# A six-layer window-attention stack: the closing normalization moves to ScalarE, and the planner gets other durations, delays and priorities

## The chip, the core and the metric

The kernel runs on one core of a Trainium2 chip. The core has a matrix engine (TensorE, PE in the profile, with its weight loads shown apart as PEld), a vector engine (VectorE, DVE), an activation engine (ScalarE, ACT), a general-purpose engine (GpSimd, POOL) and a queue that issues the transfers (SyncE, SP). Each engine works through its own list of instructions in order. An instruction that needs the result of another engine waits for a semaphore, and everything behind it on its engine waits too. The metric is device time in microseconds (us), the median of several runs. The profile comes from one execution with the hardware profiler on.

## What is computed

Sixteen sequences of 256 tokens, 128 features wide, all in 32-bit floats, go through four blocks, each followed by a residual sum and a normalization over the features. The first three blocks (linear attention, a mixture of eight experts, a causal attention with softmax feature maps) form the first stage of the kernel, which the change doesn't touch. The fourth block is the six-layer stack. Cut to what matters:

```python
def attn_layer(x, Wqkv, qs, ksc, Wo):              # 16 heads of 64
    q, k, v = split(x @ Wqkv)
    q, k = l2norm(q) * qs, l2norm(k) * ksc
    q = q * cos * scale + rotate_half(q) * sin * scale
    k = k * cos / scale + rotate_half(k) * sin / scale
    out = local_attention(q, k, v)                 # each block of 32 sees itself and the block before
    return out @ Wo
def ffn_layer(x, g, bln, W1, b1, W2, b2):
    xn = normalized(x) * g + bln
    a, gate = split(xn @ W1 + b1)
    return a * gelu(gate) @ W2 + b2
for i in range(6):
    x = attn_layer(shift_tokens(x), ...) + x
    x = ffn_layer(shift_tokens(x), ...) + x
out = _layernorm(x_in + x)                         # the closing normalization
```

## The kernel before

**Units and tiles.** Two sequences make a unit, so there are 8 units; a sequence has two tiles of 128 tokens, so a unit has 4. The stack keeps each unit's activations in SBUF for all six layers, transposed (features on partitions), in `xs`.

**Two stages.** The first stage, planned by a `Plan` of its own, ends near 1085 us of the span. The second stage is the stack: for each layer, each unit: two sequences through `projections`, `rotations`, `windows`, `attention` and `output`, then one `feed_forward` for the unit. After the last layer each unit goes through `final`, which transposes it back, adds the kept input and normalizes it.

**The planner.** The program isn't written in the order in which it runs. Every piece of work is a `Step` with an engine, a duration in us (`work`), the steps that must come first, the buffers it takes and those it uses. `Plan.run` is a list scheduler on the host: it steps through a modelled time; whenever an engine is free it issues, of the steps whose predecessors are done in the model and whose buffers are free, the one with the lowest rank. A step counts as done `work` plus the engine's `LAG` after its start. The rank is the number of the tile (so older tiles go first) plus a due time by kind plus an entry of the dictionary given to `Plan` (a negative entry makes a kind of step more urgent; 1.0 is worth one tile). The durations, delays and ranks decide nothing at run time. They decide the order in which each engine's instructions are written down, and which buffer each step gets. The chip then runs that order with its own durations and waits.

**Buffers that bind.** The stack shares four PSUM buffers of two banks each (`pair`) between all products, transposes and mixes; five `t1` and two `t2` buffers hold the two halves of the rotation, and `final` takes one of each from its first step to its last.

**One tile, with the lines of the profile.** The projection (L1086, two for a tile: q and k) writes a `pair`. Three steps read it: `second` (VectorE, L1100), `first` (VectorE, L1093) and `square` (ScalarE, L1107). The model has no dependency among these three readers. `squares` (L1113) sums the squares, `rotated` (GpSimd, L1110) adds the two halves, `norms` (GpSimd, L1063 to L1071) makes the inverse norms, `scale` (GpSimd, L1156) applies those of k. `turn` (L1160) transposes on TensorE, `put` (L1166) copies out on ScalarE. `scores` (L1234), then `mask` (L1242) and `top` (L1256) on VectorE, `below` on GpSimd (L1264), `exps` on ScalarE (L1268, four groups of four heads), `total` on VectorE (L1275, L1276), `divide` on GpSimd (L1279), `turn` on VectorE (L1283), `mix` on TensorE (L1293, into two `pair` buffers) and its `put` on ScalarE (L1302). `output` is L1341 and L1350, `windows` L1210 and L1213, `feed_forward` L1367 to L1434. `join` multiplies the value and output weights of a layer ahead of time.

**The end.** `final` of a unit gathers on ScalarE (L1542), transposes on TensorE (L249), adds on VectorE (L1551), takes statistics on VectorE (L1557, L1559), the inverse root on GpSimd (L1563, L228), normalizes on VectorE (L1568, four instructions of 128x128) and writes out through SP (L1574).

Of the kernel before, what the change touches and what calls it, by code (L numbers as in the profile page):

```python
# [16 lines left out]
P = 128  # L17
# [182 lines left out]
def tile_kernel(ctx: ExitStack, tc: tile.TileContext, a: dict, out: bass.AP):  # L200
# [26 lines left out]
    def rsqrt(o, i, n):  # L227
        pool.tensor_tensor(o, i, nhalf.to_broadcast([P, n]), ALU.pow)  # L228
# [759 lines left out]
    with ExitStack() as st:  # L988
# [26 lines left out]
        for kT in slots["kT"]:  # L1015
# [6 lines left out]
            "attention.divide": 0.5,  # L1022
            "attention.below": 8,
            "projections.first": 0.5,
# [3 lines left out]
            "windows.turn": 3,  # L1028
# [6 lines left out]
            "attention.exps": 4.5,  # L1035
            "feed_forward.turn_back": -6,
            "attention.total": 1.5,
            "feed_forward.inner": 2,
            "join.product": 1,
            "attention.put": 4,  # L1040
            "rotations.scale": 2,
        })

# [104 lines left out]
        def rotations(q):  # L1148
# [21 lines left out]
            nm = step("pool", 5.3, norms, q.reds, [], [q.ss], q.rank + due["norms"])  # L1170
# [4 lines left out]
        def turned(q, t, nm, scale, turn, put):  # L1175
# [5 lines left out]
            for qk in range(2):  # L1181
# [4 lines left out]
                else:  # L1186

                    m = o.adds[qk]
                tn = step("pe", 0.95, partial(turn, o.t1s[qk], pz), [m], [pz], [o.t1s[qk]], rank + due["rotated"], count=16)
# [3 lines left out]
                        "act", 0.91, partial(put, dst, off, pz), [tn], new,  # L1193
# [6 lines left out]
        def windows(q):  # L1200
# [15 lines left out]
            tn = step("pe", 0.5, turn, [*q.ready, begun], [pz, q.xw], [], rank + due["windows"], count=8)  # L1216
            q.spread = step("act", 0.6, put, [tn], [], [pz, q.xw], rank)

        def attention(q, t):
# [93 lines left out]
            mk = step("dve", 1.13, mask, sc, [e], [pS], rank + due["mask"])  # L1313
            tp = step("dve", 1.13, top, [mk], [], [e], rank + due["top"])
            be = step("pool", 0.35, below, [tp, o.normed], [], [], rank)
            ex = [step("act", 1.36, partial(exps, g), [be], [], [e], rank, ("exp", 0)) for g in range(4)]
            q.soft.append(tp)
            sm = step("dve", 1.46, total, ex, [], [e], rank)
            dv = step("pool", 1.87, divide, [sm], [], [e], rank)
            te = step("dve", 1.24, turn, [dv], [eT], [e], rank + due["turn"])  # L1320
            if t == 0:
# [4 lines left out]
                "pe", 2.27, partial(mix, ps), [te, q.spread, *q.mixed], [*ps, *new],  # L1326
# [3 lines left out]
            for g in range(2):  # L1330
                q.outs.append(
                    step("act", 0.91, partial(put, g, ps[g]), [mx], [], [ps[g], q.zT], rank)
                )
# [22 lines left out]
        def feed_forward(u, w, after, loaded, rank):  # L1356
# [80 lines left out]
            sx = step("dve", 1.3, stats, [tn], [], [px], rank)  # L1437
# [5 lines left out]
            for c in range(len(FCH)):  # L1443
                pg = Buf("pair")
                gm = step("pe", 0.92, partial(inner, 1, c, pg), [af], [pg], [xn], rank + due["ff_inner"])
# [79 lines left out]
        def final(u, after, rank):  # L1525
# [7 lines left out]
            def tile_of(b, j):  # L1533
                return half(b, 1)[:, j * P : (j + 1) * P]
# [141 lines left out]
```

## Time and profile before

| What | us |
|---|---|
| median of 3 runs | 4286.88 (4279.67 to 4288.96) |
| the profiled execution | 4283.78 |
| its span, first to last instruction | 4281.5 |
| TensorE busy | 4026.8 (94%) |
| VectorE busy | 3540.7 (83%) |
| ScalarE busy | 3147.6 (74%) |
| GpSimd busy | 2692.0 (63%) |
| first stage, about | 0 to 1085 |

The mean granted TensorE clock of the execution is 0.988 of full speed. The transfers are few: 37.03 MB over the whole span, a mean of 9 GB/s.

The page lists busy time by engine, a strip of 40 slices, the queues, the chain of work that ended last, and the groups of instructions with their idle time before and who ended it. Beside it the trace can be asked for waits between pairs of lines, for the instructions in order of time, and for busy times in chosen windows. A useful clock for the second stage is the first instruction of `outer` in `feed_forward` (L1422), once for a unit and layer, 48 times in all. The starts in the second layer are at 1873.73, 1941.05, 2005.20, 2068.64, 2133.26, 2197.61, 2261.95 and 2326.29 us, and in the last layer at 3941.76, 4009.06, 4087.69, 4157.76, 4218.76, 4250.92, 4260.72 and 4268.03 us.

### The profile page before, as it was taken

How to read it: one execution, taken by the hardware profiler on the slowest of the kernel's cores; microseconds unless marked ns; L12 is line 12 of the kernel's file. 1: busy time of each engine (PE TensorE's matmuls, PEld its weight loads, DVE VectorE, ACT ScalarE, POOL GpSimd, SP SyncE). 2: the span in 40 equal slices, each digit the busy share in tenths (PEclk: the TensorE clock that was granted, in tenths of full speed). 3: DMA queues.
4: the chain of work that ended last, by engine and by line, in shares of the span. 5: the costliest groups of instructions: out<-in, count | busy, mean ns of one | idle time of the engine just before them, and what ended most of it. 6: DMA issues, size and time to landing. Idle time of an engine off the chain costs nothing.

```text
span 4281.5 us, 104658 instructions
## 1 busy us (share of the span) xinstructions
PE 4026.8 (94%) x43728; PEld 2666.5 (62%) x43728; DVE 3540.7 (83%) x5201; ACT 3147.6 (74%) x6106; POOL 2692.0 (63%) x2865
## 2 busy tenths in 40 slices
PE   8999999999799999999999999999999999999888
PEld 5777777787455555565565565565555565555555
DVE  6888888787688888888888888888888888888886
ACT  6766766665478778787778777778787787777675
POOL 2654555566676676667666666766666666766662
PEclk9999999999899999999999999999999999999999
DMA  3000000000000000000000000000000000000000
GB/s 89 4 6 6 4 1 4 3 4 3 20 2 11 2 13 2 7 12 2 13 2 7 11 2 13 2 7 12 2 13 2 7 12 2 2 2 4 9 7 25
DMA packets 30836, 37.03 MB, mean 9 GB/s; under 512 B 5406, under 2 KB 24348, under 8 KB 29596
## 3 DMA queue, kind: packets, MB, share of 16 engines
q1 hardware_dynamic: 30364, 30.35, 2.4%
q8 instruction: 343, 5.62, 0.6%
q14 instruction: 129, 1.06, 0.1%
HBM read 26.15 MB, written 4.19 MB: 7 GB/s over the span
## 4 chain that ended last, share of the span: by engine, by line
PE 54%; DVE 25%; POOL 9%; ACT 8%; issue 4%; SPq 0%; DMA 0%; ACTq 0%; POOLq 0%; DVEq 0%
PE pp L1086 10%; PE pp L1341 8%; PE pp L1160 6%; DVE d_t L1093 5%; DVE d_t L1100 5%; PE pp L1402 4%; ACT d_sq L1107 4%; PE pp L1293 4%; DVE d_e L1242 3%; POOL d_e L1279 3%; PE pp L1234 3%; POOL d_t L1110 2%; PE pp L1422 2%; PE pb L665 2%; DVE d_eT L1283 2%
## 5 line engine op out<-in xcount | busy, mean ns | idle before, releaser
L1110 POOL TENSOR_TENSOR d_t<-d_t,d_t 128x1024 f32<-128x1024 f32 x384 | 904.4, 2360 | 770.0 <-DVE d_t L1093 734.1
L1268 ACT ACTIVATE d_e<-d_e,d_m,d_ny 128x64 f32<-128x64 f32 x3072 | 1071.3, 433 | 90.6 <-POOL d_m L1264 90.0
L1086 PE MATMUL pp<-d_wqkv,xs 128*128 128x512 f32 x1536 | 731.8, 609 | 12.5 <-DVE d_e L1242 6.7
L1341 PE MATMUL pp<-d_zT,d_wvo 128*128 128x256 f32 x3072 | 685.7, 381 | 7.5 <-DVE d_t L1093 2.8
L1100 DVE TENSOR_TENSOR d_t<-pp,d_tab 128x1024 f32<-128x1024 f32 x384 | 467.4, 1218 | 220.6 <-ACT d_sq L1107 126.9
L1341 PEld LDWEIGHTS pp<-d_zT,d_wvo 128*128 128x128 f32 x3072 | 577.8, 191 | 89.5 <-ACT d_sq L1107 8.6
L1107 ACT ACTIVATE d_sq<-pp 128x1024 f32<-128x1024 f32 x384 | 389.0, 1022 | 313.6 <-DVE d_t L1093 102.8
L1302 ACT COPY d_zT<-pp 128x1024 f32<-128x1024 f32 x384 | 373.2, 1012 | 235.1 <-PE pp L1293 235.1
L1093 DVE TENSOR_TENSOR d_t<-pp,d_tab 128x1024 f32<-128x1024 f32 x384 | 465.4, 1213 | 61.7 <-ACT d_sq L1107 61.6
L1113 DVE TENSOR_REDUCE d_ss<-d_sq 128x16 f32<-128x1024 f32 x384 | 455.0, 1201 | 6.4 <-ACT d_sq L1107 5.2
L1293 PE MATMUL pp<-d_eT,d_xw 32*128 32x512 f32 x3072 | 434.1, 618 | 26.2 <-ACT f_xn L1396 17.2
L1160 PE MATMUL pp<-ident,d_t 128*128 128x128 f32 x3072 | 409.4, 280 | 49.3 <-DVE d_t L1093 30.7
L1086 PEld LDWEIGHTS pp<-d_wqkv,xs 128*128 128x128 f32 x1536 | 276.2, 192 | 272.5 <-issue 225.2
L1234 PEld LDWEIGHTS pp<-d_kT,d_qT 64*32 64x32 f32 x24576 | 238.6, 106 | 329.8 <-issue 296.1
L1160 PEld LDWEIGHTS pp<-ident,d_t 128*128 128x128 f32 x3072 | 340.9, 143 | 144.2 <-issue 57.7
L1279 POOL TENSOR_TENSOR d_e<-d_e,d_z 128x1024 f32<-128x1024 f32 x192 | 365.1, 1902 | 46.5 <-DVE d_z L1276 43.0
L1156 POOL TENSOR_TENSOR d_t<-d_t,d_ny 128x1024 f32<-128x1024 f32 x192 | 363.2, 1903 | 0.4
L855 POOL TENSOR_TENSOR c_e<-c_e,c_sm 128x1024 f32<-128x1024 f32 x128 | 248.7, 1950 | 178.1 <-DVE c_sm L851 125.0
L1234 PE MATMUL pp<-d_kT,d_qT 64*32 64x64 f32 x24576 | 333.6, 224 | 8.0 <-ACT d_kT L1166 4.5
L1283 DVE STREAM_TRANSPOSE d_eT<-d_e 128x1024 f32<-128x1024 f32 x192 | 237.6, 1238 | 105.3 <-POOL d_e L1279 105.2
L1402 PE MATMUL pp<-f_xn,d_w 128*128 128x512 f32 (+1 forms) x576 | 276.5, 605 | 29.5 <-DVE d_e L1242 27.8
L1293 PEld LDWEIGHTS pp<-d_eT,d_xw 32*128 32x128 f32 x3072 | 156.4, 184 | 186.8 <-issue 87.8
(184 smaller groups left out, 7252.5 us busy)
## 6 DMA issues: line engine op xcount, KB each, us to landing
d_wqkv<-L_ffn_Wqkv SPq DMA_DIRECT2D x6, 1024.0 KB
d_t<-L_ffn_Wqkv SPq DMA_DIRECT2D x10, 256.0 KB
d_t<-L_ffn_Wo SPq DMA_DIRECT2D x10, 256.0 KB, 3.5
a_xin<-L_attn_x SPq DMA_DIRECT2D x8, 256.0 KB, 2.9
keep<-bc_x SPq DMA_DIRECT2D x8, 256.0 KB, 2.0
d_t<-keep SPq DMA_DIRECT2D x8, 256.0 KB, 3.9
out<-d_t SPq DMA_DIRECT2D x8, 256.0 KB, 2.3
d_w<-L_ffn_W SPq DMA_DIRECT2D x6, 341.0 KB
```

Of the source, the lines that this page charges most:

```text
L1086: pe.matmul(pj.t[:, hf * 512 : (hf + 1) * 512], lhsT=xj, rhs=q.w["qkv"][:, c : c + 512], start=True, stop=True,)
L1093: dve.tensor_tensor(t1.t, heads(pj.t), bc(q.lay.tab[:, 0, t, cc], hs, 1), ALU.mult)
L1100: dve.tensor_tensor(t2.t.rearrange("p h (x d) -> p h x d", x=2), swapped(pj.t), bc(q.lay.tab[:, 1, t, cc].rearrange("p (x d) -> p x d", x= ...
L1107: act.activation(sq.t, heads(pj.t), AF.Square)
L1110: pool.tensor_tensor(t1.t, t1.t, t2.t, ALU.add)
L1113: dve.tensor_reduce(q.ss.t[:, t, qk, :], sq.t, AX.X, ALU.add)
L1160: pe.transpose(pz.t[:, c * P : (c + 1) * P], t1.t[:, 2 * c : 2 * c + 2, :].rearrange("p h d -> p (h d)"), ident,)
L1234: pe.matmul(pS.t[b * WIN : (b + 1) * WIN, s0 : s0 + 2 * WIN], lhsT=qT.t[r, c, b * WIN : (b + 1) * WIN], rhs=kT.t[r, c, k0 : k0 + 2 * WIN], ...
L1268: act.activation(each()[:, h, :], each()[:, h, :], AF.Exp, bias=o.m[:, h : h + 1], scale=norm_of(h),)
L1279: pool.tensor_tensor(each(), each(), bc(o.z, es, 2), ALU.mult)
L1293: pe.matmul(ps[b // 2].t[:, (b % 2) * 512 : (b % 2 + 1) * 512], lhsT=q.xw.t[r, 2 * t + j, :], rhs=eT.t[r, j, :, :].rearrange("p h n -> p ( ...
L1341: pe.matmul(pr.t[:, :SEQ], lhsT=q.w["vo"][:, (h % 2) * 8 + h // 2, :], rhs=q.zT.t[:, :, h, :], start=(h == 0), stop=(h == HEADS - 1),)
```

## The change

The change has two parts, both in the second stage.

The last step of `final` moves: four `tensor_scalar` instructions on VectorE (subtract the mean, multiply by the inverse root) become four `activation` instructions on ScalarE with the function Identity (scale by the inverse root, add a bias). The bias, minus mean times inverse root, is made by two more small instructions on GpSimd.

The second planner gets another table of priorities, other delays, and other durations for some steps. The first planner keeps all of its own.

```diff
             "attention.mix": -0.5,
-            "attention.divide": 0.5,
-            "attention.below": 8,
-            "projections.first": 0.5,
+            "attention.divide": 2.5,
+            "attention.below": 11,
+            "projections.first": -1.0,
...
-            "windows.turn": 3,
+            "windows.turn": 3.5,
...
-            "attention.exps": 4.5,
+            "attention.exps": 7.5,
             "feed_forward.turn_back": -6,
-            "attention.total": 1.5,
+            "attention.total": 3.0,
             "feed_forward.inner": 2,
-            "join.product": 1,
-            "attention.put": 4,
-            "rotations.scale": 2,
+            "attention.put": 6,
+            "rotations.scale": 3,
+            "projections.square": -0.5,
         })
+        plan.LAG = {"pe": 0.12, "act": 0.1, "dve": 0.13, "pool": 0.1, "sp": 2.5}
```

Before, `LAG` was pe 0.27, act 0.17, dve 0.2, pool 0.1, sp 2.5. The durations, old and new, in us:

| step | engine | old | new |
|---|---|---|---|
| `rotations.norms` | GpSimd | 5.3 | 5.2 |
| `rotations.turn` | TensorE | 0.95 | 1.0 |
| `rotations.put` | ScalarE | 0.91 | 0.9 |
| `windows.turn`, `windows.put` | TensorE, ScalarE | 0.5, 0.6 | 0.55, 0.5 |
| `attention.mask` | VectorE | 1.13 | 1.19 |
| `attention.below` | GpSimd | 0.35 | 0.25 |
| `attention.exps` | ScalarE | 1.36 | 1.34 |
| `attention.total`, `attention.turn` | VectorE | 1.46, 1.24 | 1.42, 1.17 |
| `attention.mix` | TensorE | 2.27 | 2.05 |
| `attention.put` | ScalarE | 0.91 | 0.9 |
| `feed_forward.stats`, `gated`, `add` | VectorE | 1.3, 0.7, 1.55 | 1.06, 0.66, 1.46 |
| `feed_forward.inner`, `outer` | TensorE | 0.92, 2.58 | 0.87, 2.67 |
| `final.gather` | ScalarE | 1.1 | 1.26 |
| `final.root` | GpSimd | 1.32 | 1.9 |
| `final.normal` | VectorE, then ScalarE | 1.4 | 1.3 |

And the moved step:

```diff
             def root():
                 o.rs = sd.tile([P, TPU], F32, name="f_rs")
+                o.nb = sd.tile([P, TPU], F32, name="f_nb")
                 pool.tensor_scalar(o.rs, o.mv[:, :, 1], EPS, None, ALU.add)
                 rsqrt(o.rs, o.rs, TPU)
+                pool.tensor_tensor(o.nb, o.mv[:, :, 0], o.rs, ALU.mult)
+                pool.tensor_scalar(o.nb, o.nb, -1.0, None, ALU.mult)
 
             def normal():
                 for j in range(TPU):
-                    dve.tensor_scalar(
-                        tile_of(b2, j), tile_of(b1, j), o.mv[:, j, 0:1], o.rs[:, j : j + 1],
-                        ALU.subtract, ALU.mult,
+                    act.activation(
+                        tile_of(b2, j), tile_of(b1, j), AF.Identity,
+                        bias=o.nb[:, j : j + 1], scale=o.rs[:, j : j + 1],
                     )
```

## The prediction

> **What bounds the kernel now.** I read the busy line and the chain first.
>
> ```profile
> PE 4026.8 (94%) x43728; PEld 2666.5 (62%) x43728; DVE 3540.7 (83%) x5201; ACT 3147.6 (74%) x6106; POOL 2692.0 (63%) x2865
> PE 54%; DVE 25%; POOL 9%; ACT 8%; issue 4%; SPq 0%; DMA 0%; ACTq 0%; POOLq 0%; DVEq 0%
> ```
>
> TensorE is nearly always occupied, yet holds only half of the chain: VectorE carries a quarter. So I looked at one unit of the stack. The starts of `outer` (L1422) repeat every 64.34 us in the middle of each layer. A table of busy time over one such unit and over two of the last layer:
>
> ```profile
> core 0: us, PE busy (x) PEld busy (x) DVE busy (x) ACT busy (x) POOL busy (x), PEclk, DMA share, GB/s
> 2586.09:2650.43 64.34, 61.39 (x771) 37.11 (x770) 54.73 (x66) 50.24 (x96) 43.97 (x50) 1.00 0.06 20
> 4009.06:4087.69 78.63, 70.31 (x797) 43.11 (x795) 63.88 (x88) 51.61 (x94) 44.76 (x53) 0.93 0.03 8
> 4087.69:4157.76 70.07, 61.98 (x756) 38.19 (x755) 61.24 (x70) 52.64 (x104) 45.84 (x51) 0.93 0.03 9
> ```
>
> A steady unit leaves TensorE 64.34 - 61.39 = 2.95 us idle and VectorE 9.6. The list of TensorE's waits inside that unit names 2.6 us of this, in four places:
>
> ```profile
> PE pp L1210 <- DVE d_t L1093: 0.8, 1, 0.8
> PE pp L1402 <- DVE d_e L1242: 0.8, 1, 0.8
> PE pp L1160 <- DVE d_t L1093: 0.6, 1, 0.6
> PE pp L1293 <- ACT f_xn L1396: 0.4, 1, 0.4
> ```
>
> Two of the four end when `first` (L1093) releases a `pair` buffer. TensorE is the bound, but the stalls left in it are set by when VectorE empties PSUM. VectorE in turn waits for ScalarE at the same buffer, over the whole span:
>
> ```profile
> DVE d_t L1100 <- ACT d_sq L1107: 126.9, 103, 6.7
> DVE d_t L1093 <- ACT d_sq L1107: 61.6, 53, 1.6
> ```
>
> The planner models no order among `second`, `first` and `square`; on the chip the readers of one `pair` run one after the other, in the order in which the plan issued them.
>
> The last layer has a loss of its own. Its third and fourth units take 78.63 and 70.07 us, 14.3 + 5.7 = 20.0 above 64.34. In order of time, VectorE and then GpSimd near 4043 us, and VectorE at the very end:
>
> ```profile
> 4042.99 5.89 DVE L1568 TENSOR_SCALAR d_t<-d_t,f_mv,f_rs 128x128 f32<-128x128 f32 x4 [0.78 <-POOL f_rs L228]
> ...
> 4042.93 1.90 POOL L1156 TENSOR_TENSOR d_t<-d_t,d_ny 128x1024 f32<-128x1024 f32 x1
> 4044.78 1.90 POOL L1279 TENSOR_TENSOR d_e<-d_e,d_z 128x1024 f32<-128x1024 f32 x1
> 4046.64 1.90 POOL L1156 TENSOR_TENSOR d_t<-d_t,d_ny 128x1024 f32<-128x1024 f32 x1
> ...
> 4277.09 1.11 DVE L1568 TENSOR_SCALAR d_t<-d_t,f_mv,f_rs 128x128 f32<-128x128 f32 x4 [1.47 <-POOL f_rs L228]
> ```
>
> The same four instructions take 1.11 us when GpSimd is idle and 5.89 while it runs three large operations. Of the eight units four (near 3967, 4043, 4113 and 4193 us) take 5.9; TensorE then waits 2.97 and 2.27 us near 3973 and 3983, and 5.12 near 4050.
>
> **The moved step.** Removed from VectorE: 4 x 5.9 + 4 x 1.11 = 28 us, of which only what falls into the two long units can reach the end. I take their two slow passes, 2 x 5.9 = 12 us of the 20.0; the rest of the excess may belong to the other steps of `final`, which stay, and to the two `t2` buffers of which `final` holds one. Bounds: nothing, if GpSimd's or the buffers' order sets those units; 20 us, if the stall sets off all of it.
>
> Added on ScalarE: 32 instructions of 128x128. The nearest row is the expert stage's activation of this size with a scale by partition (L674, 370 ns): 4 x 0.37 = 1.5 us for a unit. ScalarE is busy 51.6 of 78.6 us there, which hides it; without that cover it costs 4 x 1.5 = 6 us in the units that aren't in the drain. Behind it on ScalarE stand `exps`, `square` and `put` of younger tiles, so a late root would hold them; L1568 waited for the root 3.7 us in all eight units, and that is the price. A table load needn't come: the Identity at L1396 shows none of its own among the groups, only L1268's and L1409's.
>
> The Trainium skill (ScalarE: Activation LUTs, Rules for kernel authors) speaks against this move: adds and multiplies belong on VectorE. Its section What ACT_TABLE_LOAD costs would give, as an estimate, 280 + 0.833 x 128 + 93 - 93 = 387 ns per instruction, 1.55 us for four against VectorE's undisturbed 1.11, a loss of 8 x 0.44 = 3.5 us of engine time. By the trace the rule holds in the drain only; beside GpSimd's work the row reads 5.89.
>
> Added on GpSimd: two instructions per unit. By the nearest rows, L1069 (319 ns) and L1563 (0.23 us) with 0.08 of issue each, 0.71 us; GpSimd is busy 45 of 70 us, which hides it, except in the last unit. There the chain runs statistics, root, normalization: +0.71 for the two, and 1.48 - 1.11 = 0.37 for the slower engine: **+1.1 us at the end**. The write-out on SP waits for ScalarE instead of VectorE; behind it on SP stands only the next unit's fetch of its kept input (256 KB, 3.9 us to landing), which an older `final` has time for until the drain.
>
> **The durations and delays.** They cost no instruction; they change the order. What they are worth depends on whether the model then reads more like the chip. Start to start of dependent steps, where the second engine was waiting: projection to `square` 2503.13 to 2505.05 = 1.92 us (model 1.82 + 0.27 = 2.09 before, 1.94 after); `mix` to `put` 2568.24 to 2570.27 = 2.03 (2.54, 2.17); `turn` to `put` 2553.25 to 2554.38 = 1.13 (1.22, 1.12); `exps` to `total` 2587.52 to 2588.98 = 1.46 (1.53, 1.44); `square` to `second` 2505.05 to 2506.17 = 1.12 (1.09, 1.02). Four of five come closer. A unit has 8 projections, 4 mixes and 8 turns: 8 x 0.17 + 4 x 0.51 + 8 x 0.09 = 4.1 us of `pair` time that the old plan held back and the chip didn't need.
>
> **The priorities.** `first` goes from 0.5 to -1.0 and `square` from 0 to -0.5: the projection's PSUM is emptied earlier. `exps`, `total`, `divide`, `below`, `scale` and the puts go one to three tiles later; `join.product` one earlier, with its transfers where they were. Of TensorE's four gaps the ones ended by `first` are those that this can shorten: 0.81 + 0.61 = 1.42 us a unit. `mask` and the affine step that end the other two keep their priorities. I take half, 0.71, since the same move also sends ScalarE and VectorE to one buffer at once (below). Bounds: a gain of the whole 2.6, a loss of 2.0 (last rival). From the second `outer` of the first layer (1423 us) to the fourth of the last (4158 us) are 42 units: 42 x 0.71 = **30 us**. The fill (TensorE idle 36 us between 1000 and 1200) and the drain could move by 10 us either way; I take nothing.
>
> **Sum.** Span 4281.5 - 30 - 12 + 1 = 4240.5. The median of the runs lies 5.4 above the profiled span (the profiled execution itself 2.3): **4246 us**.
>
> **Rivals.** *Collision at the projection's buffer (slower).* If `square` and the two VectorE readers now always become ready together, each projection costs VectorE the 1.15 us wait that single cases show (2544.29, 2608.92), against 188.5 / 384 = 0.49 now: 8 x 0.66 = 5.3 us more idle VectorE a unit. Today 9.6 us of VectorE idle go with 2.2 of TensorE idle behind VectorE, a share of 0.23: 5.3 x 0.23 x 42 = 51 us, less 11: 4327. For: 156 such waits already. Against: `second` at -3 already goes first. It decides once it costs 11 / 42 = 0.26 us a unit, when the two waits grow from 188 to about 240 us.
>
> *The steady unit stays at 64.3.* Then only `final` counts: 4286.9 - 11 = 4276. For: TensorE is 95% busy in it. Against: the order changes everywhere.
>
> *All of TensorE's named waits go.* 42 x 2.6 = 109, with 11 more: 4167. Against: it needs VectorE never late.
>
> *Late puts hold PSUM (slower).* `mix` takes two of four `pair` buffers; if its put comes one ScalarE instruction (1.0 us) later for 4 tiles and half of that reaches TensorE, 2.0 x 42 = 84, less 11: 4360. Against: ScalarE waits 235 us for `mix` at L1302, so puts are early now.
>
> **How the numbers follow.** Forecast 0.48; collision 0.20; unchanged unit 0.12; all waits gone 0.08; late puts 0.12. About 0.2% (8.6 us) can be told from no change. Faster: the forecast, all waits gone and half of the unchanged unit, 0.62. Same: 0.07, from the unchanged unit and a weak collision. Slower: 0.31. The forecast's own range is 4190 to 4278. For 8 in 10 the range takes in the collision and part of the full gain: 4172 to 4340.
>
> **What would show it.** The distance between `outer` starts in mid-layer: 63.6 us instead of 64.34. The third and fourth units of the last layer, 148.7 us together: under 138. Four normalizations on ScalarE at about 1.5 us wherever they fall. VectorE's waits for `square`: under 188 us or little above. I am wrong if the unit is longer than 64.34, or if TensorE's waits turn to PSUM copies on ScalarE.

## The result and the profile after

The changed kernel takes 4319.65 us (median of four runs, 4314.31 to 4322.71) beside 4285.34 for the kernel before (four runs). The ratio is 1.0079 with a 95% interval of 1.0064 to 1.0094, so the change costs 34 us, where 41 were forecast as a gain. In the second stage every line down to the change in `final` stands one further down than before: `first` is L1094, `second` L1101, `square` L1108, the projection L1087, `outer` L1423.

The busy line and the chain of the changed kernel:

```profile
PE 4053.2 (94%) x43728; PEld 2686.8 (62%) x43728; DVE 3518.0 (81%) x5169; ACT 3161.0 (73%) x6140; POOL 2701.9 (63%) x2881
PE 43%; DVE 34%; ACT 13%; POOL 5%; issue 4%; SPq 0%; DMA 0%; ACTq 0%; DVEq 0%; POOLq 0%
```

TensorE's share of the chain fell from 54% to 43%. VectorE and ScalarE took it: 34% and 13%, from 25% and 8%. The three readers of a projection (`second`, `first`, `square`) hold 20% of the chain, from 14%.

The table of busy time, over one steady unit in mid-layer and over the fourth unit of the last layer (columns: stretch, length, then busy time and instructions of each engine, granted clock, DMA share, GB/s):

```profile
core 0: us, PE busy (x) PEld busy (x) DVE busy (x) ACT busy (x) POOL busy (x), PEclk, DMA share, GB/s
2606.98:2672.54 65.56, 62.27 (x770) 37.86 (x771) 54.97 (x66) 50.19 (x97) 44.12 (x50) 1.00 0.06 20
...
4122.04:4187.89 65.85, 62.28 (x766) 37.53 (x766) 54.19 (x73) 51.95 (x98) 42.86 (x52) 1.00 0.04 13
```

A steady unit grew from 64.34 to 65.56 us: TensorE's idle time from 2.95 to 3.29, its busy time from 61.39 to 62.27 with the same matmuls. The last layer went the other way: its units after the first `outer` took 65.91, 66.99 and 65.85 us, where they had been 67.30, 78.63 and 70.07.

By the starts of `outer` the whole difference of the two spans, 4316.9 - 4281.5 = 35.4, splits up: the second `outer` comes 2.5 us earlier (1420.64 against 1423.10); the 39 units from there to the last layer cost 49.8 us more, 1.28 each; the three long units give back 17.3; from the fourth `outer` of the last layer to the end it is 129.0 us instead of 123.7, 5.3 more. The 39 units and the three long ones, first before, then after:

```profile
1423.10:3941.76 2518.66, 2404.72 (x30192) 1466.07 (x30191) 2135.01 (x2533) 1968.20 (x3744) 1719.14 (x1957) 1.00 0.02 6
3941.76:4157.76 216.00, 193.07 (x2304) 118.55 (x2303) 186.35 (x226) 156.58 (x300) 136.43 (x155) 0.94 0.03 9
```

```profile
1420.64:3989.14 2568.50, 2435.61 (x30200) 1486.94 (x30199) 2142.14 (x2534) 1969.07 (x3754) 1725.98 (x1959) 1.00 0.02 6
3989.14:4187.89 198.75, 187.81 (x2314) 114.67 (x2314) 166.83 (x221) 158.81 (x302) 134.56 (x160) 1.00 0.04 11
```

In the 39 units TensorE's idle time grew by 19.0 us (113.9 to 132.9) and its busy time by 30.9. Of the 17.3 us that the three long units give back, 12.0 are idle time (22.9 to 10.9) and 5.3 busy time. The granted clock in them rose from 0.94 to 1.00, which the busy time would show; why it was lower before no run separates.

TensorE's waits inside that steady unit (us in total, times, longest):

```profile
PE pp L1211 <- DVE d_t L1094: 1.1, 1, 1.1
PE pp L1403 <- ACT f_h L1410: 0.7, 1, 0.7
PE pp L1161 <- DVE d_t L1094: 0.7, 1, 0.7
PE pp L1087 <- ACT d_kT L1167: 0.6, 1, 0.6
```

The two that `first` ends were 0.81 + 0.61 and are now 1.1 + 0.7, though `first` had been made more urgent. Over the 39 units, though, the sum of TensorE's waits that `first` ends hardly changed, 60.6 to 61.9 us. What grew there are the waits that ScalarE ends, 17.5 to 52.9, while those that VectorE ends fell from 90.2 to 66.7. The longest of those 39 units, first before, then after:

```profile
PE pp L1210 <- DVE d_t L1093: 37.1, 44, 1.1
PE pp L1402 <- DVE d_e L1242: 27.0, 29, 1.1
PE pp L1160 <- DVE d_t L1093: 17.4, 28, 0.9
PE pp L1293 <- ACT f_xn L1396: 16.3, 34, 0.7
```

```profile
PE pp L1211 <- DVE d_t L1094: 33.3, 30, 1.3
PE pp L1403 <- ACT f_h L1410: 25.3, 35, 0.7
PE pp L1087 <- ACT d_kT L1167: 22.1, 34, 0.9
PE pp L1161 <- DVE d_t L1094: 20.4, 30, 0.7
```

The waits at the shared buffer, over the span:

```profile
DVE d_t L1101 <- ACT d_sq L1108: 195.3, 144, 6.9
...
ACT d_sq L1108 <- DVE d_t L1101: 179.7, 159, 3.3
...
DVE d_t L1094 <- ACT d_sq L1108: 97.2, 85, 1.2
...
ACT d_sq L1108 <- DVE d_t L1094: 20.4, 13, 2.5
```

VectorE's waits for `square` grew from 188.5 to 292.5 us, ScalarE's at `square` for the two VectorE readers from 176 to 200. In order of time (start, duration, engine, instruction; in brackets the idle time before it and who ended it) one such case runs through to TensorE:

```profile
2632.04 1.23 DVE L1101 TENSOR_TENSOR d_t<-pp,d_tab 128x1024 f32<-128x1024 f32 x1
...
2633.36 1.03 ACT L1108 ACTIVATE d_sq<-pp 128x1024 f32<-128x1024 f32 x1 [0.22 <-DVE d_t L1101]
...
2634.42 1.23 DVE L1094 TENSOR_TENSOR d_t<-pp,d_tab 128x1024 f32<-128x1024 f32 x1 [1.15 <-ACT d_sq L1108]
...
2635.70 0.66 PE L1211 MATMUL pp<-ident,xs 128*128 128x128 f32 x4 [1.11 <-DVE d_t L1094]
```

Three readers of one `pair`, two engines, one after the other: `second`, `square`, `first`. VectorE stands still for the 1.15 us of `square`, and the transpose of `windows` for 1.11 until the buffer is free. The model that made this order lets `second` and `square` run at once. The Trainium skill (PSUM — Partial Sum Buffer, section PSUM bank collisions raise a hardware error) says that accesses of two engines to one bank and group of partitions, two reads included, have to be kept apart by software. The trace agrees as far as it goes: the waits are there between readers, with no write among them. What happens without the waits no run here shows.

### The profile page after: what moved, and what is told of

It is laid out like the page before. It is cut to its first block, busy times and chain, and to the rows that moved or that the text cites. A ratio compares the mean times of both kernels' runs of the same rounds, so it can differ in the third digit from the quotient of the medians.

```text
span 4316.9 us, 104683 instructions
## 1 busy us (share of the span) xinstructions
PE 4053.2 (94%) x43728; PEld 2686.8 (62%) x43728; DVE 3518.0 (81%) x5169; ACT 3161.0 (73%) x6140; POOL 2701.9 (63%) x2881
## 3 DMA queue, kind: packets, MB, share of 16 engines
q14 instruction: 130, 1.06, 0.1%
## 4 chain that ended last, share of the span: by engine, by line
PE 43%; DVE 34%; ACT 13%; POOL 5%; issue 4%; SPq 0%; DMA 0%; ACTq 0%; DVEq 0%; POOLq 0%
DVE d_t L1101 8%; PE pp L1342 8%; ACT d_sq L1108 6%; DVE d_t L1094 6%; PE pp L1087 6%; PE pp L1403 4%; PE pp L1294 3%; PE pp L1161 3%; PE pp L1235 3%; DVE d_ss L1114 2%; PE pb L665 2%; DVE d_m L1257 2%; PE pb L874 2%; ACT d_e L1269 2%; ACT d_zT L1303 2%
## 5 line engine op out<-in xcount | busy, mean ns | idle before, releaser
L1087 PE MATMUL pp<-d_wqkv,xs 128*128 128x512 f32 x1536 | 733.2, 607 | 31.0 <-ACT d_kT L1167 22.1
L1101 DVE TENSOR_TENSOR d_t<-pp,d_tab 128x1024 f32<-128x1024 f32 x384 | 468.9, 1221 | 218.3 <-ACT d_sq L1108 195.3
L1108 ACT ACTIVATE d_sq<-pp 128x1024 f32<-128x1024 f32 x384 | 392.2, 1025 | 311.4 <-DVE d_t L1101 179.7
L1094 DVE TENSOR_TENSOR d_t<-pp,d_tab 128x1024 f32<-128x1024 f32 x384 | 464.7, 1211 | 98.9 <-ACT d_sq L1108 97.2
L1087 PEld LDWEIGHTS pp<-d_wqkv,xs 128*128 128x128 f32 x1536 | 273.9, 191 | 320.2 <-issue 222.0
L1294 PE MATMUL pp<-d_eT,d_xw 32*128 32x512 f32 x3072 | 433.8, 617 | 10.9 <-DVE d_t L1094 4.2
L1161 PEld LDWEIGHTS pp<-ident,d_t 128*128 128x128 f32 x3072 | 339.5, 143 | 124.5 <-issue 49.8
L1403 PE MATMUL pp<-f_xn,d_w 128*128 128x512 f32 (+1 forms) x576 | 289.3, 623 | 35.2 <-ACT f_h L1410 27.1
L1276 DVE TENSOR_REDUCE d_z<-d_e 128x16 f32<-128x1024 f32 x192 | 232.7, 1212 | 65.4 <-ACT d_e L1269 65.2
```

The lines of the kernel that those rows point to most:

```text
L1087: pe.matmul(pj.t[:, hf * 512 : (hf + 1) * 512], lhsT=xj, rhs=q.w["qkv"][:, c : c + 512], start=True, stop=True,)
L1094: dve.tensor_tensor(t1.t, heads(pj.t), bc(q.lay.tab[:, 0, t, cc], hs, 1), ALU.mult)
L1101: dve.tensor_tensor(t2.t.rearrange("p h (x d) -> p h x d", x=2), swapped(pj.t), bc(q.lay.tab[:, 1, t, cc].rearrange("p (x d) -> p x d", x= ...
L1108: act.activation(sq.t, heads(pj.t), AF.Square)
L1161: pe.transpose(pz.t[:, c * P : (c + 1) * P], t1.t[:, 2 * c : 2 * c + 2, :].rearrange("p h d -> p (h d)"), ident,)
L1294: pe.matmul(ps[b // 2].t[:, (b % 2) * 512 : (b % 2 + 1) * 512], lhsT=q.xw.t[r, 2 * t + j, :], rhs=eT.t[r, j, :, :].rearrange("p h n -> p ( ...
```

## The experiments

Each kernel ran beside the kernel before on the same chip. Times are medians; the interval is that of the ratio to the kernel before.

### The two parts of the change, alone

`final_only` is the kernel before with the moved normalization (the second diff of the change, and its durations 1.9 and 1.3). `plan_only` is the changed kernel without it.

```diff
-            no = step("dve", 1.4, normal, [rt], [], [b1, b2], rank)
+            no = step("act", 1.3, normal, [rt], [], [b1, b2], rank)
```

> The kernel before with the closing normalization on ScalarE and nothing else (root 1.9 and normal 1.3 in the plan). Collision theory (the loss comes from the order of the three readers of a projection's PSUM buffer, the move of the normalization gains): the third and fourth unit of the last layer fall from 148.7 us together to about 133, steady unit stays 64.3, time about 4270 (4264 to 4277). Rival, the normalization itself costs (it stands in ScalarE's queue ahead of exps and square, and lengthens the drain by the 4 us by which the changed kernel's drain is longer): 4285 or more.

> The changed kernel with the closing normalization back on VectorE (durations 1.32 and 1.4): only durations, delays and priorities are new. Collision theory: steady unit 65.6 us as in the changed kernel, time about 4335 (4325 to 4345), above the changed kernel by what the move gained. Rival, the move of the normalization is the loss: back near 4285.

`final_only` took 4275.29 against 4281.59, 0.9985 (0.9975 to 0.9994): a gain of 6 us. `plan_only` took 4329.51, 1.0111 (1.0096 to 1.0126): a loss of 48. So the two parts have opposite signs, and the loss is all in the planning. In `plan_only` the steady unit is 65.55, as in the changed kernel, and the last layer's units are 67.1, 75.3 and 70.4. In `final_only` they are 70.5, 66.4 and 66.4, with 12.2 us of TensorE's idle time where the kernel before had 22.9, and a granted clock of 0.98:

```profile
3942.72:4146.00 203.28, 191.07 (x2324) 115.96 (x2323) 169.86 (x223) 159.91 (x306) 137.23 (x162) 0.98 0.03 9
```

The end of `final_only`, in order of time:

```profile
4267.20 0.20 POOL L1566 TENSOR_TENSOR f_nb<-f_mv,f_rs 128x4 f32<-128x4 f32 x1
4267.49 0.24 POOL L1567 TENSOR_SCALAR f_nb<-f_nb 128x4 f32<-128x4 f32 x1
4267.77 1.65 ACT L1571 ACTIVATE d_t<-d_t,f_nb,f_rs 128x128 f32<-128x128 f32 x4 [4.77 <-POOL f_nb L1567]
```

From the end of the statistics (4265.62) to the end of the normalization (4269.42) it is 3.80 us, where the kernel before took 4278.20 - 4275.61 = 2.59: 1.21 more, as the two GpSimd instructions and the slower engine had been priced. And over the whole span, the line of the moved instructions in the changed kernel and in the one before (shortest, median and longest of the 32, in ns):

```profile
L1572 ACT ACTIVATE d_t<-d_t,f_nb,f_rs x32: 477/482/494, 4007.5 to 4313.2; 128x128 f32<-128x128 f32 x32
```

```profile
L1568 DVE TENSOR_SCALAR d_t<-d_t,f_mv,f_rs x32: 333/344/1943, 3966.9 to 4277.9; 128x128 f32<-128x128 f32 x32
```

On ScalarE none is slow; on VectorE the same work varies by a factor of nearly six.

### Which part of the planning

```diff
prio_only: the kernel before, with the change's table of priorities
dur_only: the changed kernel with the old table, without the moved normalization
after_first_back: the changed kernel, with two entries taken back
-            "projections.first": -1.0,
+            "projections.first": 0.5,
...
-            "projections.square": -0.5,
```

> The kernel before with the new table of priorities alone; old durations, old delays, normalization on VectorE. So far: with the shared PSUM reads taken away the two orders still differ by 1.25 us a unit (60.27 and 61.52), as with them (64.34 and 65.56). Theory A, the priorities make that difference: steady unit 65 us or more, time 4310 to 4340. Theory B, the shorter durations and delays make it (steps planned too tightly, TensorE finds inputs just late): unit about 64.3, time 4275 to 4295. The planner's own modelled unit here is 63.1 to 63.8, against 62.6 for the kernel before, so it too takes these priorities for worse under the old durations.

> The kernel before with the new durations and delays alone; old priorities, normalization on VectorE. Theory A (priorities): unit about 64.3, time 4270 to 4295. Theory B (too tight durations and delays): unit 65 or more, time 4310 or more. The modelled unit is 62.4, against 62.6 before.

> The changed kernel with two entries of the table undone: first back at 0.5, square without an entry. The prediction's collision rival put the loss on these two. If that is so: VectorE's waits for square fall from 292 us towards 188, unit near 64.3, time 4270 to 4290. If not: unit near 65.6, time 4310 to 4330 whatever the waits do.

`prio_only` took 4335.79, 1.013 (1.0115 to 1.0145). `dur_only` took 4330.32, 1.0113 (1.0098 to 1.0128). `after_first_back` took 4326.78, 1.0109 (1.0094 to 1.0124), with the same steady unit, 65.56. Each half of the planning costs some 50 us by itself, and both together no more. The two entries that the prediction had argued from, `first` and `square`, are not the cause. `dur_only` also speaks against a plain count of waits: VectorE waits only 131.6 us for `square` there, less than before, and it is as slow.

By the starts of `outer` the same 39 units show where each half loses, first `prio_only`, then `dur_only`, and two of TensorE's longest waits in `dur_only`:

```profile
1434.27:3997.58 2563.31, 2440.99 (x30192) 1481.16 (x30191) 2126.25 (x2528) 1986.06 (x3751) 1725.26 (x1958) 1.00 0.02 6
```

```profile
1423.80:3989.25 2565.45, 2411.60 (x30173) 1488.05 (x30172) 2133.07 (x2520) 1974.98 (x3740) 1722.08 (x1955) 1.00 0.02 6
```

```profile
PE pp L1161 <- ACT d_zT L1303: 28.2, 29, 1.2
PE pp L1294 <- ACT d_sq L1108: 26.1, 29, 1.5
```

The new table alone adds 36.3 us of TensorE's busy time and 8.4 of idle time; the new durations and delays alone add 6.9 and 39.9. So the priorities lose mostly in busy time, which with equal matmuls is a matter of their order, and the durations in waits: TensorE now waits 26.1 us for `square` and 36.5 for the put of the mix, against next to nothing before. In both kernels a few of the units ran at a granted clock below 1, which is a part of the busy time.

### Without the shared read

The third reader is taken off the `pair`: `square` squares the query weights in SBUF, of the same size. It then no longer waits for the projection either (94.4 us of ScalarE's time over the span before), and no longer holds the buffer. The norms of q and k are then not those of the projection.

```diff
-                act.activation(sq.t, heads(pj.t), AF.Square)
+                act.activation(sq.t, heads(q.w["qkv"][:, :INNER]), AF.Square)
```

> The kernel before, with square reading 1024 columns of the layer's query weights in SBUF in place of the projection in PSUM (the norms of q and k are left uncomputed): same order, same work, but ScalarE no longer shares a PSUM buffer with VectorE. Collision theory: VectorE's waits for square at the two rotation lines go from 188 us to near 0, unit 64.3 falls to about 62.5 to 63.5, time 4210 to 4250. Rival (late puts and delayed exps): the time falls little, by under 20 us.

> The changed kernel with the same replacement (square reads query weights in SBUF, the norms are left uncomputed). Collision theory: waits go from 292 us to near 0, and the changed order turns out better than the old one, as its own planner thought (modelled unit 61.2 against 62.6): unit about 62, time 4150 to 4200, at least 20 us below the kernel before with the same replacement. Rival (late puts, too short delays): it stays 20 to 50 us above the kernel before with the same replacement.

Before: 4108.2, 0.9594 (0.958 to 0.9609). After: 4125.57, 0.9633 (0.9619 to 0.9647). A steady unit of each, first the kernel before, then the changed one:

```profile
3048.61:3108.87 60.26, 60.01 (x772) 36.98 (x771) 54.53 (x66) 50.08 (x97) 45.33 (x52) 1.00 0.01 2
```

```profile
3064.61:3126.14 61.53, 61.38 (x771) 37.39 (x771) 54.61 (x66) 50.05 (x97) 44.63 (x51) 1.00 0.01 2
```

The third read, with its wait for the projection and its hold on the buffer, costs 4.1 us of a steady unit in the old order and 4.0 in the new one, more than all of TensorE's idle time there (2.95 and 3.29). But 1.27 us of difference stay without it, and there TensorE has 0.25 and 0.15 us of idle time left: that difference is in the order of the matmuls themselves. Over the 39 units (2375.57 us before, 2407.03 after) 31.5 of the 49.8 us stay without the third read (41.7 more busy time, 10.2 less idle time), and 18 go with it. So the waits at the buffer are not the whole loss. I had looked for 4210 to 4250 and 4150 to 4200, with the changed order the faster of the two: a miss on all three.

### The order on TensorE

From the records I counted TensorE's time by groups of equal matmuls. In every plan a unit has 57.88 us of matmuls at their own spacing. The rest is idle time, stalls inside a group, and a surplus at the change from one group to another: 3.01, 0.89 and 2.56 us before with 39 groups, 3.29, 0.85 and 3.54 after with 42. How the stalls divide between the last two is a matter of my count; the 57.88 and those two together are TensorE's busy time, which the rows show. The surplus is largest where a few 128x128 matmuls stand between two groups of the 64x32 `scores`: 0.15 us around a transpose, 0.20 around a product. In the kernel before, eight transposes take 1.02 us from their start to the scores behind them (2592.87 to 2593.89), and 0.93 to a product behind them (2596.58 to 2597.51). The glue kernels write the second group of scores of a tile directly behind the first where one other group lay between (197 places after, 189 before).

```diff
+            if a.kind == b.kind == "attention.scores" and b in a.next and m.kind in ("turned.turn", "rotations.turn", "projections.product", "windows.turn"):
+                pe[k + 1], pe[k + 2] = b, m
+                follow[a] = b
```

> The changed kernel's plan, with one thing done to TensorE's list after planning: where a single transpose, product or window turn stands between two groups of scores of the same tile, the second group is put straight behind the first (197 places, 4.3 a unit). Nothing else is moved. By the traces a steady unit of the changed kernel spends 3.54 us in changes from one kind of TensorE work to another, that before 2.56, and a transpose between two score groups costs 0.15 us more than one that isn't, a product 0.20. Theory that these changes are the loss: the unit falls from 65.56 to 64.6 to 65.0, time down by 20 to 45 us, to 4275 to 4300. Theory that waits for other engines set the unit (the time saved turns into waiting): within 8 us of 4320.

> The kernel before with the same treatment of TensorE's list (189 places, 4.1 a unit). If the changes of work cost TensorE in this order as well: unit from 64.34 to 63.5 to 63.9, time 4240 to 4265. If the order is bound by VectorE's late release of PSUM: within 8 us of 4282, idle of TensorE grows by what the changes lose.

After: 4327.07, 1.0106 (1.0089 to 1.0123). Before: 4277.37, 0.999 (0.998 to 0.9999). In the changed kernel the surplus fell from 3.54 to 3.24 us of a unit and the idle time rose from 3.29 to 3.98: what the switches gave went into waits. The surplus is real, but it isn't the cause that can be taken away by itself.

### Another order of the readers, by hand

The pairs kernels write `first` ahead of `square` wherever `first` directly follows `second` on VectorE's list and `square` lay between (84 places after, 51 before), so that VectorE reads twice without a stop.

```diff
+            if a.kind == "projections.second" and b.kind == "projections.first" and a.pair is b.pair:
+                if where[a] < mid[a.pair] < where[b]:
+                    follow[a] = b
```

> The changed kernel's plan, with one thing done after planning: where VectorE's list has first straight behind second of the same projection and square stands between them in the program's order, first is written ahead of square (84 places, 1.8 a unit). Every engine keeps its own list; only the order in which the three readers of one PSUM buffer follow one another changes, from second, square, first to second, first, square. Theory that the order of the readers is the loss: VectorE's 97 us of waits at first nearly vanish, the unit falls from 65.56 to 64.5 to 65.3, time down by 10 to 45 us. Theory that it isn't: the waits vanish and the time stays within 8 us of 4320.

> The kernel before with the same treatment (51 places, 1.1 a unit). Theory that the order of the readers sets the unit: the 62 us of waits at first nearly vanish, time down by 5 to 25 us. Otherwise within 8 us of 4281.

After: 4435.54, 1.0338 (1.0315 to 1.0362). Before: 4344.99, 1.0137 (1.012 to 1.0154). Both are slower, which neither of my readings had. Some 1.4 and 1.2 us are lost at each place. A part is the clock: some units of both ran at a granted clock of 0.95 to 0.98. By the units at full clock (67.86 against 65.56, 65.54 against 64.34) it is 1.3 and 1.1 us a place. In the first of the two, the waits over the span:

```profile
DVE d_t L1120 <- ACT d_sq L1127: 222.1, 146, 6.9
ACT d_sq L1127 <- DVE d_t L1113: 216.6, 96, 4.4
```

VectorE's waits at `first` are gone, but ScalarE's for `first` rose from 20.4 to 216.6. ScalarE holds its list in order too, so `exps` and the puts stand behind a `square` that waits. In these two plans the order could not be mended at one buffer afterwards.

### The planner told of the shared read

Here only the model is changed. Two of the three readers on different engines may no longer overlap on one `pair`; nothing else about the steps or the chip is touched.

```diff
+                        if s.lock and s.lock.held > now + 1e-6:
+                            back.append(item)
+                            continue
...
+                    if got.lock:
+                        got.lock.held = now + work + self.LAG[eng]
...
-                a1 = step("dve", 1.13, partial(first, qk, pj, t1), [mm, q.tabbed], [], [pj, t1], rank)
+                a1 = step("dve", 1.13, partial(first, qk, pj, t1), [mm, q.tabbed], [], [pj, t1], rank, lock=pj)
```

The same `lock=pj` goes to `second` and `square`. It was put into the changed kernel (`after_lock`), the kernel before (`before_lock`) and `dur_only` (`dur_lock`).

> The changed kernel, whose planner is told that first, second and square exclude each other on one PSUM buffer (a step may not start in the model before the reader before it has ended and its delay has passed); same priorities, durations, normalization on ScalarE. The modelled unit becomes 64.3. Theory that the orders lose because they are planned blind to the shared reads: unit 63.5 to 64.5 on the chip, time 4240 to 4280. Theory that the loss lies elsewhere: unit 65 or more, time 4310 or more.

> The kernel before (old priorities, old durations and delays) with the planner that knows the shared reads. Modelled second stage 3227 us: by the same sum 4317 (4295 to 4340), slower than before although it knows more, because the old durations and the longer delays make it leave engines idle in the model. If knowing the shared reads always helps, under 4270.

> dur_only (old priorities, new durations and delays, normalization on VectorE) with a planner that knows that first, second and square exclude each other. Its modelled second stage is 3099 us, against 3173 for after_lock, which took 4262.6 on the chip: if the planner that knows the shared reads ranks orders as the chip does, 4262.6 - 3172.8 + 3099.3 = 4189 (4170 to 4215), 140 us under dur_only. If what an order is worth isn't a matter of the shared reads, it stays at 4260 or more.

`after_lock` took 4262.64, 0.9962 (0.9949 to 0.9974): by the ratios some 50 us less than the changed kernel (1.0079), and faster than the one before. `before_lock` took 4232.03, 0.9877 (0.9858 to 0.9897); I had looked for 4317 there, a miss. `dur_lock` took 4174.46, 0.9748 (0.9733 to 0.9762). In `dur_lock` a steady unit, TensorE's one wait in it, and VectorE's and ScalarE's waits over the span:

```profile
3108.29:3169.04 60.75, 60.36 (x773) 37.38 (x771) 54.10 (x66) 50.07 (x97) 45.48 (x52) 1.00 0.01 2
```

```profile
PE pp L1410 <- ACT d_zT L1310: 0.3, 1, 0.3
```

```profile
DVE d_t L1108 <- ACT d_sq L1115: 48.9, 86, 6.7
...
ACT d_sq L1115 <- DVE d_t L1101: 3.8, 4, 2.4
ACT d_sq L1115 <- DVE d_t L1108: 3.2, 6, 1.5
```

TensorE is idle for 0.39 us of the unit. The waits at the shared buffer sum to 56 us, from 277 in `dur_only` and 493 in the changed kernel: the readers still run one after the other, but the plan now has other work in between. Over the 39 units TensorE's idle time is 22.4 us (2409.02 - 2386.59), from 153.9 in `dur_only`. Other units in mid-layer take up to 61.9 us; the mean of the 39 is 61.8.

### The square filled, and a table of priorities for this model

`lag_lock` is `before_lock` with the new delays and the old durations, `prio_lock` is `before_lock` with the new priorities, `final_dur_lock` is `dur_lock` with the normalization on ScalarE.

```diff
lag_lock
+        plan.LAG = {"pe": 0.12, "act": 0.1, "dve": 0.13, "pool": 0.1, "sp": 2.5}
```

> The kernel before with two things: the shared reads known to the planner, and the new delays between engines; old durations, old priorities, normalization on VectorE. before_lock (old delays) took 4232.0, dur_lock (new delays and new durations) 4174.5. If the delays bring it, this is near 4180 to 4195; if the durations do, near 4230. The modelled ends are 3227.5, 3157.6 and 3099.3, which by the mean offset of before_lock and dur_lock (1004.5 and 1075.2, so 1040) would give 4197.

> The kernel before with the new priorities and the shared reads known to the planner; old durations and delays, normalization on VectorE. With before_lock (4232.0), dur_lock (4174.5) and after_lock (4262.6, some 6 less for its normalization on ScalarE) it fills the square of priorities by durations. If the new priorities cost by themselves about 94 us (4268.6 - 4174.5) whatever the durations: 4232 + 94 = 4326. If it was the pairing of priorities and durations that cost there: near 4232 or below.

> The changed kernel with the old priorities and the planner told that first, second and square of one PSUM pair exclude each other: the normalization on ScalarE, which the run dur_lock had on VectorE, is the only difference from it. If the moved normalization is worth here what it was alone, 6 us (4281.6 to 4275.3): 4174.5 - 6 = 4168. The rival is the plan: its modelled end comes 6.7 us later than dur_lock's (3106.0 against 3099.3), which would give 4181. By the theory that the new priorities are what is left of the damage, it stands some 95 us under the run after_lock (4262.6), which differs from it in the priorities alone.

`lag_lock` took 4192.27, 0.9787 (0.9772 to 0.9801): of the 58 us from `before_lock` to `dur_lock` the delays bring about 39 (0.9877 to 0.9787), the durations the rest. `prio_lock` took 4253.13, 0.9927 (0.9911 to 0.9944), 21 us above `before_lock`: of my two readings, one had put the cost of the new priorities at 94 us there too, the other near nothing, and it lies between. `final_dur_lock` took 4182.64, 0.9762 (0.9747 to 0.9777), not told apart from `dur_lock` by the intervals; the moved step gains nothing in this plan.

`new_prio_lock` is `final_dur_lock` with another table, found by a search over the planner's own model with the shared read in it. Its largest moves:

```diff
-            "projections.product": -9,
+            "projections.product": -13.5,
...
-            "attention.divide": 0.5,
+            "attention.divide": -19,
...
-            "attention.exps": 4.5,
+            "attention.exps": 44.5,
...
+            "projections.square": -40,
```

> The run final_dur_lock with other priorities and nothing else: a table found by a search over the planner's model with the shared reads in it, the change's durations and delays kept. Modelled end 3035.9 against 3106.0 for final_dur_lock, which took 4182.6: offset 1076.6, and 4112 if it holds. If a table that is best by the model loses on the chip even with the shared reads known, as the change's own table did without them, it stands at or above 4183. Its modelled steady unit is 61.7 us in every unit; final_dur_lock's 62.2 measured 60.7, so TensorE, with 57.9 us of matmuls and some 2.4 of switches, leaves at most some 0.5 us below that: 60.2 would be the bound, and most of the gain has to come from the starts of layers and the last units.

It took 4120.79 us, 0.9618 (0.9602 to 0.9634): 164 us under the kernel before, the fastest of the kernels here that compute the whole reference. Its busy line and one steady unit:

```profile
PE 3946.2 (96%) x43728; PEld 2678.5 (65%) x43728; DVE 3483.6 (85%) x5169; ACT 3161.1 (77%) x6138; POOL 2698.5 (65%) x2881
```

```profile
3073.39:3134.83 61.44, 59.79 (x772) 37.89 (x771) 54.16 (x66) 50.41 (x97) 44.04 (x50) 1.00 0.01 2
```

The gain isn't in the middle: the 39 units take 2403.9 us, where `final_dur_lock` has 2407.6 (its units vary from 60.7 to 61.9 in mid-layer). The 58.9 us between the two spans come from the beginning (the second `outer` at 1408.61 instead of 1436.31, 27.7), from the last layer's three units (21.2 of the 24.9 between there and its fourth `outer`) and from the drain (6.4).

### The model against the chip

The planner has a modelled end of its own for the second stage. Beside the spans, and with the difference of the two; the first stage, which the model of the second leaves out, ends near 1085:

| kernel | model knows the shared read | durations, delays | modelled end | span | difference |
|---|---|---|---|---|---|
| before | no | old | 3091.2 | 4281.5 | 1190 |
| `prio_only` | no | old | 3124.9 | 4334.6 | 1210 |
| `dur_only` | no | new | 3086.8 | 4328.0 | 1241 |
| `plan_only` | no | new | 3034.1 | 4329.0 | 1295 |
| after | no | new | 3028.7 | 4316.9 | 1288 |
| `before_lock` | yes | old | 3227.5 | 4230.9 | 1003 |
| `prio_lock` | yes | old | 3238.7 | 4254.0 | 1015 |
| `lag_lock` | yes | old, new | 3157.6 | 4191.6 | 1034 |
| `dur_lock` | yes | new | 3099.3 | 4171.4 | 1072 |
| `final_dur_lock` | yes | new | 3106.0 | 4179.9 | 1074 |
| `after_lock` | yes | new | 3172.8 | 4257.9 | 1085 |
| `new_prio_lock` | yes | new | 3035.9 | 4121.0 | 1085 |

With the shared read and the change's durations and delays, four plans come out within 13 us of each other, close to the 1085. With the old durations and delays the model is 70 to 82 us too long, without the shared read 105 to 210 us too short. The kernel before had both errors, of opposite sign: its padded hand-offs left room for a wait that the model didn't know.

## Why the prediction was wrong

**The moved step: right in kind, off in size.** -12 and +1.1 were forecast. Alone it measured -6 (by the ratio's interval, 3 to 11), in the changed plan it was -10 by the medians (4319.65 against 4329.5 for `plan_only`, on another chip) and -14 by the ratios. By the starts of `outer` in `final_only` the last layer's three units gave 12.7 back and the way from there to the end took 3.0 more instead of 1.1. Four normalizations take 1.65 us, forecast 1.5. The third and fourth units of the last layer together were to be under 138 and are 132.8. That the pass on VectorE takes 5.89 us beside GpSimd's work was read correctly from one row. The stall was the right term: 10.7 of the 12.7 are TensorE's idle time. The other 2.0 are busy time, for which the -12 had no term, though the table gave the two long units a clock of 0.93.

**The failed steps: "The durations and delays", and "The priorities" with their -30.** The sum has no term of its own for the durations and delays; they were put at nothing or better. The step went: four of five hand-offs of the model come closer to the chip, so 4.1 us of `pair` time a unit are held back that "the chip didn't need". The first half is true, as the last four rows of the table show. The conclusion is not. By themselves the new durations and delays cost 49 us, 39.9 of it in TensorE's waits in the 39 units, with new ones behind `square` and the put of the mix. The chip did need that time, for readers that the model thought parallel. The same exchange of durations and delays, with all else equal, cost 49 us in the blind model (4280.8 to 4330.3) and gained 58 in the model that knew the shared read (4232.0 to 4174.5), where TensorE's waits are nearly gone. I had the missing fact in hand (the prediction says that the planner models no order among the three readers) and used it only for a rival, not as a condition on this step.

**The priorities.** I took half of the two gaps ended by `first`, 0.71 us of 1.42, for 42 units: the -30. In the steady unit they grew to 1.8; over the 39 units the waits that `first` ends went from 60.6 to 61.9, and to 86.6 with the new table alone. Nothing was gained, and the 39 units became 49.8 us longer. A more urgent entry moves a step in the model's order; it doesn't make it ready earlier on the chip. The change's table costs 55 us in the blind model with old durations (`prio_only`), 21 with the shared read known (`prio_lock`), and some 86 beside the new durations (0.9962 against 0.9762). The planner with the shared read sees the last two (modelled +11 and +67). The blind one, beside the new durations, sees a gain of 53 (3086.8 to 3034.1); with the old ones it too sees a loss (3091.2 to 3124.9). A table that is best by a wrong model is not good by the right one.

**The bound that I read.** The steady unit was read from its named waits, 2.6 us. Of the 1.22 us that it grew, 0.34 are idle time and 0.88 are in TensorE's busy time, which I had taken as fixed; over the 39 units it is 19.0 and 30.9 of 49.8. Which matmuls stand beside which is also a result of the plan.

**The rivals.** The collision at the projection's buffer came nearest in number: 4327 forecast, 4319.65 measured, its threshold of 240 us passed with 292.5, 51 us of loss by its price and 49.8 measured in the units. VectorE's waits did grow as it said, but its price is luck. It takes TensorE's idle time behind VectorE to grow with them, and that fell from 90.2 to 66.7 us in the 39 units; the growth is behind ScalarE, and the larger part of the loss is busy time. Nor does the count of waits order the plans: `dur_only` has 131.6 us of them and is as slow, `new_prio_lock` 152.7 and is 4% faster. The late puts (4360) named the right engine: TensorE's waits did turn to ScalarE's readers of PSUM. That and the longer unit were the two signs that I had named for being wrong. In the changed kernel they are the `gelu` (L1410, 25.3 us) and the put of k (L1167, 22.1), not the put of the mix, which the rival had priced; that one shows in `dur_only`, with 36.5. The unchanged unit and the vanished waits are out.

**What stays open.** Taking away the third read takes 18 of the 49.8 us of the units, about as much as idle time grew, and leaves 31.5, about as much as busy time grew. What in the order of the matmuls costs the 31.5 isn't shown: gluing the scores moved their share into idle time. A plan with as much room left elsewhere, in place of the shared read, was not tried, so it is four pairs of plans, each faster by 50 to 156 us, that speak for the rule itself. Undoing two entries of the table (`after_first_back`) moved the time by 13 us by the ratios, so a difference of that size between two plans says little about one entry. The blind model with the new delays and old durations was not tried, nor the best table with the normalization on VectorE.

## What to carry to other kernels

When an order is planned from a model, better numbers help only if the model has every resource that binds. Padding in an old model may stand for a rule that nobody wrote down, so before tightening durations, compare the modelled end with the measured one for two or three plans, and look in the trace for waits between steps that the model thinks independent. Here some lines for two engines that read one PSUM buffer were worth 50 to 156 us, and turned a loss of 49 us into a gain of 58.

## What the runs showed of the hardware

The four-instruction normalization ran at 477 to 494 ns an instruction on ScalarE wherever it fell, and at 333 to 1943 ns on VectorE. The Trainium skill (SBUF — State Buffer, section Who interferes with whom) gives VectorE and GpSimd a shared port pair, which in some of VectorE's modes one of them locks for a whole instruction, and ScalarE ports of its own. The rows agree with that.

I had not expected the price of order on TensorE: with equal matmuls, TensorE's busy time of a steady unit is 59.79 us in `new_prio_lock`, 60.36 in `dur_lock`, 61.39 before and 62.27 in the changed kernel. Nor that a single turned pair of readers would cost 1.1 to 1.3 us at full clock, about a whole instruction, at each place where it was done.
